# Twelve rounds of zero products between the biases' products and the first x products of a GRU kernel

## The chip, the cores and the metric

The kernel runs on one core of a Trainium2 chip. The metric is the device time of one execution in microseconds. The runs of the kernel before took 1161.91, 1162.43 and 1162.65 us, a median of 1162.43. TensorE (PE) does the matrix products, and its weight loads are shown as an engine of their own (PEld). VectorE (DVE), ScalarE (ACT) and GpSimd (POOL) do the elementwise work. SyncE (SP), ACT and POOL issue the transfers.

## The reference

x has 16 sequences of 256 steps with 512 values. A GRU runs over the steps with one state of 512 values for each sequence. An expert layer with top-k choice over all 4096 tokens follows, and its result is added to x.

```python
def cell(h, x):
    gi = x @ W_ih + b_ih
    gh = h @ W_hh + b_hh
    i_r, i_z, i_n = jnp.split(gi, 3, axis=-1)
    h_r, h_z, h_n = jnp.split(gh, 3, axis=-1)
    r = jax.nn.sigmoid(i_r + h_r)
    z = jax.nn.sigmoid(i_z + h_z)
    n = jnp.tanh(i_n + r * h_n)
    h_new = (1.0 - z) * n + z * h
    return (h_new, h_new)
...
logits = xf @ router_w + router_b
S = jax.nn.softmax(logits, axis=-1)
G, idx = jax.lax.top_k(S.T, k)
tokens = xf[idx]
out = jnp.einsum('ekh,hd->ekd', tokens, expert_w) + expert_b
weighted = G[..., None] * out
y = jnp.zeros((bs, h), dtype=x.dtype).at[idx.reshape(-1)].add(weighted.reshape(-1, h))
...
x = x + ffn(gru(cond_2048, x))
```

Both stages are in float32. Each step needs the state of the step before it, so the 256 steps run one after another.

## The kernel before

**Tiling.** The 512 columns of a gate are split into four parts of 128 (KC = 4). A product for 16 or 32 rows uses 32 columns of the TensorE array, so four of them, one for each quadrant j, stand side by side and write to PSUM partitions 32j to 32j + 31. Steps are taken in pairs p, with an even and an odd step sharing 32 PSUM rows. Each pair has banks of its own out of six (`banks`): `ra` for the r gate and the x part of the n gate, `hn` for the h part of n, `zz` for the z gate. Eight steps make a group g.

**Set-up, before the loop.** The transfers are issued in an order written out by hand (lines 276 to 299). SP and ACT each load half of the rows of `wih` and then of `whh`, by gate in the order r, n, z. POOL loads the biases, then the first two x pairs of group 0 into `xa0`, then the first state into `c0`. SP loads the remaining two x pairs behind its halves of the weights.

On PE and DVE the order is also written by hand, in the block that the change touches. PE runs, in this order:

1. `begin_sums` (line 108) for the six banks: four products of zeros each, bfloat16, 128 rows and 512 columns. They set every bank to zero and open it for sums.
2. `keep_clock(22)`: 22 rounds of `begin_sums` on two spare PSUM banks, `idles`, which nothing reads.
3. `biases(1)` and `biases(0)` (line 303): the bias rows are spread over the quadrants by products with a column of ones. They have only one or two rows to sum over. DVE copies the result to `bias` and `nb`, from which later pairs are preset.
4. The x products of pairs 0 and 1, `x_part` (line 436): first the r and n parts with 256 columns, then the z part with 128, for four blocks k each. They read `xT`, which DVE transposes from `xa0` by `turn_x` (line 253), one pair at a time.
5. `keep_clock(2)`: two more rounds.

Meanwhile DVE transposes the first state and copies it to `hs` (lines 492 and 493).

**The loop.** For every step s, PE runs the h products (`h_part`, line 450: r and n for the first half of k, r and n for the second half, then z). ACT and DVE then work out the gates and the new state, which the next step's h products need. PE fills the wait with the x products of later pairs and with units of the expert layer. In step 1, DVE transposes the rest of `xa0`; after that, group 1's x is loaded into the same buffer. What follows the loop is the softmax, the search for the k-th largest score, and the sums and stores of the output.

Of the kernel before, what the change touches and what calls it, by code (L numbers as in the profile page):

```python
# [18 lines left out]
def kernel(  # L19
# [88 lines left out]
    def begin_sums(bank):  # L108

        n = bank.shape[-1]  # L110
        for j in range(KC):
            nc.tensor.matmul(
                bank[QD * j : QD * (j + 1)],
                zero,
                zero[:, 0:E].unsqueeze(1).to_broadcast([P, n // E, E]),
                start=True,
                stop=True,
                tile_position=(0, QD * j),
            )
# [67 lines left out]
    with (  # L187
# [65 lines left out]
        def turn_x(g, xa, pairs=slice(0, TG // 2)):  # L253
            if g not in xT:
                xT[g] = xtp.tile([P, TG // 2, P], F32, name="xt")
            nc.vector.transpose(  # L256
                xT[g][:, pairs, :].rearrange("p q (c r) -> p q c r", c=KC),
                xa[:, pairs, :].rearrange("p q (i c) -> p q c i", c=KC),
            )
# [43 lines left out]
        def biases(i):  # L303
            for dst, rows in (
                (ra[i][:, 0, :], b_raw[:, 0, :]),
                (ra[i][:, 1, :], b_raw[0:1, 2, :]),
                (hn[i][:, 0:P], b_n),
                (zz[i], b_raw[:, 1, :]),
            ):
                for j in range(KC):  # L310
                    nc.tensor.matmul(
                        dst[quadrant(j)],
                        ones[0 : rows.shape[0]],
                        columns(rows, j),
                        start=False,
                        stop=True,
                        tile_position=(0, QD * j),
                        skip_group_check=True,
                    )
# [3 lines left out]
        def of_step(ap, odd):  # L323
            return ap.rearrange("p (c q b) -> p c q b", q=2, b=B)[:, :, odd, :]
# [111 lines left out]
        def x_part(p, k, z):  # L436
            g, pair = divmod(p, TG // 2)
            lhs = xT[g][:, pair, QD * k : QD * (k + 1)]
            for j in range(KC):
                q = quadrant(j)  # L440
                dst, rhs = (
                    (zz[p % 2][q], columns(wih[:, k, 2, :], j))
                    if z
                    else (ra[p % 2][q], columns(wih[:, k, 0:2, :].rearrange("p g d -> p (g d)"), j))
                )
                nc.tensor.matmul(  # L446
                    dst, lhs, rhs, start=False, stop=(k == KC - 1), tile_position=(0, QD * j), skip_group_check=True
                )
# [22 lines left out]
        def keep_clock(n):  # L471

            for i in range(n):
                begin_sums(idles[i % 2])

        with tc.manual_schedule(engines={ET.PE, ET.DVE}):
            for bank in banks:
                begin_sums(bank)
            keep_clock(22)
            biases(1)  # L480
            biases(0)
            nc.vector.tensor_copy(bias[:, 0:2, :], ra[1])
            nc.vector.tensor_copy(nb, hn[1][:, 0:P])
            nc.vector.tensor_copy(bias[:, 2, :], zz[1])
            for pair in range(2):
                turn_x(0, xa0, slice(pair, pair + 1))
            for z in (False, True):
                for pair in range(2):
                    for k in range(KC):
                        x_part(pair, k, z)  # L490
            keep_clock(2)
            nc.vector.transpose(turned, c0)
            nc.vector.tensor_copy(hs[:, :, 0, :], of_step(turned, 0))
# [400 lines left out]
```

## Time and profile before

| | |
|---|---|
| median of 3 runs | 1162.43 us (1161.91 to 1162.65) |
| the profiled execution, its own time | 1162.4 us |
| its span, first to last instruction | 1160.5 us |
| mean granted TensorE clock | 0.996 |
| zero rounds of `keep_clock(22)`, last product ends | 9.29 us |
| biases' products (L311), PE | 9.22 to 11.18 us |
| x products of pairs 0 and 1 (L446), PE | 15.49 to 22.56 us |
| h products of step 0 (L459), PE | from 22.82 us |
| ACT's sigmoid of r in step 0 (L517) | 24.38 us |

Times within the execution are counted from the first instruction. A row of the timeline gives the start, the length, the engine, the line, the operation with its tiles (out<-in) and shapes, and how many instructions it merges; in brackets is the idle time of the engine before it and what ended it. A row of the table by stretches gives the stretch, its length, the busy time of PE, PEld, DVE, ACT and POOL with the number of instructions, then the granted TensorE clock as a share of full speed (PEclk), the share of the transfer engines and their GB/s. Each float32 product counts as two MATMUL instructions. Their ends are modelled, so their starts and the weight loads are the surer measure.

### The profile page before, as it was taken

To read this page: it belongs to the slowest core of one execution; us is meant where nothing else is said; L and a number is where in the kernel's file an instruction comes from. 1 tells how busy PE (TensorE), PEld (TensorE's weight loads), DVE (VectorE), ACT (ScalarE), POOL (GpSimd) and SP (SyncE) were. 2 spreads that over 40 slices of the span, in tenths; PEclk is the share of its full clock that TensorE was granted. 3 is DMA by queue.
4 is the path that set the end of the run, shared out by engine and by line. 5 is a ranking of instruction groups with operands and counts; after the bars stand their busy time and mean duration, and the time that the engine had idled before them with its cause. 6 is when DMAs were issued, how large, how long until landed. Compare 5 with 4: busy or idle time off the path is not lost. (4 is left out here: it accounts for less than half of the span.)

```text
span 1160.5 us, 79363 instructions
## 1 busy us (share of the span) xinstructions
PE 1145.6 (99%) x36017; PEld 1008.8 (87%) x36017; DVE 703.4 (61%) x4078; ACT 343.2 (30%) x1459; POOL 100.0 (9%) x412
## 2 busy tenths in 40 slices
PE   7999999999999999999999999999999999999998
PEld 4899999999999999999999999999999999989742
DVE  1656665666666566666665666666666666666675
ACT  0323323232333333333233322233232323343320
POOL 3000010000000000000000000000000000000000
PEclk8999999999999999999999999999999999999999
DMA  7200000000000000000000000000000000000017
GB/s 235 73 23 20 21 18 21 21 20 19 20 21 20 21 20 20 21 20 21 20 19 22 21 20 18 23 20 21 18 21 20 20 21 20 21 18 13 4 45 249
DMA packets 48854, 38.01 MB, mean 33 GB/s; under 512 B 7968, under 2 KB 40800, under 8 KB 48512
## 3 DMA queue, kind: packets, MB, share of 16 engines
q1 hardware_dynamic: 46272, 29.56, 8.6%
q8 instruction: 283, 4.64, 1.7%
q10 hardware_dynamic: 1632, 3.15, 0.8%
q14 instruction: 59, 0.48, 0.1%
q0 software_dynamic: 608, 0.19, 0.1%
HBM read 24.47 MB, written 8.39 MB: 28 GB/s over the span
## 5 line engine op out<-in xcount | busy, mean ns | idle before, releaser
L459 PE MATMUL gates<-whh,hs 128*16 128x128 f32 x24576 | 719.4, 273 | 3.5 <-DVE hs L592 2.0
L459 PEld LDWEIGHTS gates<-whh,hs 128*16 128x16 f32 x24576 | 672.2, 103 | 10.0 <-DVE hs L592 4.6
L446 PE MATMUL gates<-wih,xt 128*32 128x256 f32 (+1 forms) x8192 | 380.9, 327 | 4.4 <-DVE xt L256 4.3
L446 PEld LDWEIGHTS gates<-wih,xt 128*32 128x32 f32 x8192 | 245.2, 110 | 72.4 <-DVE xt L256 4.6
L517 ACT ACTIVATE r<-gates 128x128 f32<-128x128 f32 x256 | 70.9, 277 | 605.5 <-PE gates L459 605.5
L521 DVE COPY seen<-r 1x1 f32<-1x1 f32 x256 | 36.3, 142 | 326.8 <-ACT r L517 326.8
L571 ACT ACTIVATE t<-t 128x64 f32<-128x64 f32 x512 | 102.9, 248 | 132.6 <-DVE t L569 132.6
L578 DVE STREAM_TRANSPOSE nT<-t 128x64 f32<-128x64 f32 x512 | 100.2, 234 | 49.3 <-ACT t L571 49.3
L581 DVE STREAM_TRANSPOSE zT<-zs 128x64 f32<-128x64 f32 x512 | 121.7, 238 | 0.2 <-issue 0.2
L592 DVE TENSOR_TENSOR hs<-v,nT 128x32 f32<-128x32 f32 x512 | 101.7, 199 | 21.7
L589 DVE TENSOR_TENSOR v<-u,zT 128x32 f32<-128x32 f32 x512 | 104.4, 204 | 8.8
L407 PE MATMUL pe<-ewr,ht 128*32 128x128 f32 x1920 | 93.9, 273 | 0.0
L567 DVE TENSOR_TENSOR t<-r,gates 128x64 f32<-128x64 f32 x512 | 89.7, 217 | 0.0
L569 DVE TENSOR_TENSOR t<-t,gates 128x64 f32<-128x64 f32 x512 | 88.4, 214 | 0.0
L584 DVE TENSOR_TENSOR u<-hs,nT 128x32 f32<-128x32 f32 x512 | 78.4, 153 | 0.0
L407 PEld LDWEIGHTS pe<-ewr,ht 128*32 128x32 f32 x1920 | 59.5, 110 | 19.4
L572 ACT ACTIVATE zs<-gates 128x128 f32<-128x128 f32 x256 | 70.9, 277 | 0.0
L137 PE MATMUL pe<-ewr,ht 128*32 128x256 f32 (+1 forms) x848 | 64.3, 442 | 0.0
L622 POOL COPY xa<-hs 32x1 f32<-32x1 f32 x120 | 21.4, 179 | 478.7 <-DVE hs L592 296.7
L331 POOL COPY ht<-hs 128x128 f32<-128x128 f32 (+1 forms) x128 | 46.9, 397 | 160.2 <-DVE hs L592 152.4
L247 POOL COPY xs<-hs 1x1 f32<-1x1 f32 x128 | 22.7, 178 | 335.7 <-DVE hs L592 331.4
L137 PEld LDWEIGHTS pe<-ewr,ht 128*32 128x32 f32 x848 | 26.0, 109 | 26.2 <-issue 17.4
(102 smaller groups left out, 316.7 us busy)
## 6 DMA issues: line engine op xcount, KB each, us to landing
xs<-in_x_dram SPq DMA_DIRECT2D x128, 64.0 KB
xa<-in_x_dram SPq DMA_DIRECT2D x248, 32.0 KB
out_dram<-xs SPq DMA_DIRECT2D x31, 256.0 KB
wih<-in_L_cond_W_ih_dram SPq DMA_DIRECT2D x3, 512.0 KB
wih<-in_L_cond_W_ih_dram ACTq DMA_DIRECT2D x3, 512.0 KB
whh<-in_L_cond_W_hh_dram SPq DMA_DIRECT2D x3, 512.0 KB
whh<-in_L_cond_W_hh_dram ACTq DMA_DIRECT2D x3, 512.0 KB
ewr<-in_L_ffn_expert_w_dram SPq DMA_DIRECT2D x1, 1024.0 KB
```

Source lines behind the costliest of these rows:

```text
L137: nc.tensor.matmul(pe[q, cols], ht[:, g, k, q], ewr[:, k, E:][:, cols], start=False, stop=(k == KC - 1), tile_position=(0, QD * j), skip_g ...
L407: nc.tensor.matmul(pes[g][quadrant(j), at : at + P], ht[:, g, k, quadrant(j)], ewr[:, k, E + P * quarter : E + P * (quarter + 1)], start=F ...
L446: nc.tensor.matmul(dst, lhs, rhs, start=False, stop=(k == KC - 1), tile_position=(0, QD * j), skip_group_check=True)
L459: nc.tensor.matmul(dst[quadrant(j, m)], lhs, columns(whh[:, k, gate_, :], j), start=False, stop=(k == KC - 1), tile_position=(0, QD * j), ...
L567: nc.vector.tensor_tensor(t[half], r[:, cols], hn[p % 2][:, cols], ALU.mult)
L569: nc.vector.tensor_tensor(t[half], t[half], ra[p % 2][:, 1, cols], ALU.add)
L571: nc.scalar.activation(t[half], t[half], AF.Tanh)
L578: nc.vector.transpose(nT[half], t[half])
L581: nc.vector.transpose(zT[half], zs[:, halves[half][1]])
L584: nc.vector.tensor_tensor(u[half], hs[:, halves[half][2], slot(s), :], of_step(nT[half], odd), ALU.subtract)
L589: nc.vector.tensor_tensor(v[half], u[half], of_step(zT[half], odd), ALU.mult)
L592: nc.vector.tensor_tensor(hs[:, halves[half][2], slot(s + 1), :], v[half], of_step(nT[half], odd), ALU.add)
```

## The change

One line is added between the biases' products and the first x products, behind DVE's copies of the biases. PE's own order has the twelve rounds directly behind the last bias product. A round is `begin_sums` on one of the two spare banks, as in the 22 rounds before the biases.

```diff
@@ -482,6 +482,7 @@
             nc.vector.tensor_copy(bias[:, 0:2, :], ra[1])
             nc.vector.tensor_copy(nb, hn[1][:, 0:P])
             nc.vector.tensor_copy(bias[:, 2, :], zz[1])
+            keep_clock(12)
             for pair in range(2):
                 turn_x(0, xa0, slice(pair, pair + 1))
             for z in (False, True):
```

The functions it calls are unchanged:

```python
def keep_clock(n):
    for i in range(n):
        begin_sums(idles[i % 2])

def begin_sums(bank):
    n = bank.shape[-1]
    for j in range(KC):
        nc.tensor.matmul(
            bank[QD * j : QD * (j + 1)],
            zero,
            zero[:, 0:E].unsqueeze(1).to_broadcast([P, n // E, E]),
            start=True,
            stop=True,
            tile_position=(0, QD * j),
        )
```

`zero` is a tile of bfloat16 zeros that POOL sets once, at the start.

## The prediction

> **What bounds the kernel now.** I read the page first, for the engines and the clock. TensorE (PE) is busy for 99% of the span, the next engine for 61%. The chain of waits on the page breaks off after the last output transfer, so the order of the start has to be read from the timeline.
>
> ```profile
> PE 1145.6 (99%) x36017; PEld 1008.8 (87%) x36017; DVE 703.4 (61%) x4078; ACT 343.2 (30%) x1459; POOL 100.0 (9%) x412
> ...
> PEclk8999999999999999999999999999999999999999
> ```
>
> The reader is to see that nearly all of the run is one serial recurrence on TensorE, so time gained before its first step is kept to the end. The only slice with a granted clock below nine tenths is the first, 0 to 29 us, where the change is. Next the PE timeline there (start, us, line, tiles, count), then the DVE rows that release it:
>
> ```profile
> 9.22 1.96 PE L311 MATMUL gates<-xs,ones 2*32 2x128 f32 x64
> 15.49 7.07 PE L446 MATMUL gates<-wih,xt 128*32 128x256 f32 x128 [4.30 <-DVE xt L256]
> 22.39 0.61 PE L112 MATMUL idle<-zero 128*32 128x512 bf16 x8
> ```
>
> ```profile
> 15.03 0.40 DVE L256 STREAM_TRANSPOSE xt<-xa 128x128 f32<-128x128 f32 x1 [4.28 <-DMA xs<-in_cond_dram]
> 15.97 0.41 DVE L256 STREAM_TRANSPOSE xt<-xa 128x128 f32<-128x128 f32 x1 [0.54 <-DMA xa<-in_x_dram]
> ...
> 18.75 0.20 DVE L493 COPY hs<-nT 128x64 f32<-128x64 f32 x1
> ```
>
> After the biases' products PE has nothing to do for 4.30 us, until the first x pair is transposed. From 15.49 on, nothing but PE itself sets the end of this stretch: the second pair and the first state (18.95) are ready before PE asks for them. Last, the granted clock (PEclk is the third column from the end) over the clock's own stretches, and the weight loads, whose spacing shows the speed:
>
> ```profile
> 8.67:12.08 3.41, 2.51 (x76) 1.81 (x68) 0.82 (x3) 1.28 (x1) 2.77 (x7) 1.00 1.06 312
> 12.08:15.50 3.42, 0.01 (x2) 0.01 (x3) 0.40 (x1) 0.00 (x0) 1.51 (x6) 0.50 1.07 332
> 15.50:18.91 3.41, 3.41 (x34) 1.58 (x37) 0.89 (x4) 0.00 (x0) 0.00 (x0) 0.50 1.05 378
> 18.91:22.32 3.41, 3.41 (x100) 2.64 (x96) 0.99 (x8) 0.00 (x0) 0.30 (x1) 1.00 0.67 235
> ...
> 25.74:29.15 3.41, 2.30 (x85) 2.33 (x89) 1.89 (x14) 0.50 (x2) 0.17 (x1) 1.00 0.16 45
> ```
>
> ```profile
> 18.05 0.20 PEld L446 LDWEIGHTS gates<-wih,xt 128*32 128x32 f32 x4 [0.23 <-issue]
> 18.48 0.20 PEld L446 LDWEIGHTS gates<-wih,xt 128*32 128x32 f32 x4 [0.23 <-issue]
> 18.90 3.39 PEld L446 LDWEIGHTS gates<-wih,xt 128*32 128x32 f32 x92 [0.23 <-issue]
> ```
>
> The clock falls to half at 12.08 and comes back at 18.91, two equal stretches of 3.41 us later. So the first 3.4 us of the x products run at half speed: four loads every 0.43 us.
>
> **The change, part by part.** It adds 12 rounds of four 128x512 products, 48 of PE's 36017 matmuls, and removes and moves nothing. No semaphore of another engine stands before them: they read the zero tile and write the idle banks that the 22 rounds before have used. The DVE copies of the biases (9.93 to 10.75) run beside them. SP, ACT and POOL get no instruction, so no transfer is issued earlier or later by the change itself.
>
> *Length of the rounds.* At full speed the row "5.16, 3.64 us, x68" of the weight loads before the biases gives 3.64 / 17 = 0.214 us a round, and at half speed the rows at 4.73 and 5.16 are 0.43 apart. The bias products stop issuing at about 11.0 (loads 9.22 + 1.69, plus the last product). Twelve rounds end at 11.0 + 12 x 0.214 = 13.6 if the clock holds. If it falls at 12.08 as now, five rounds are done by then and seven take 7 x 0.43 = 3.0 us, to 15.1. Both are before 15.48, where the x products can first start. The rounds therefore cost nothing while that idle time covers them; without it they would cost 2.6 to 5.1 us.
>
> *Speed of the x products.* They are 16 passes of 256 columns, then 16 of 128. Now eight wide passes take 0.427 us (15.49 to 18.90), the other eight 0.2135 and the narrow ones 0.107: 3.42 + 1.71 + 1.71 = 6.84 us. At full speed from the start they take 16 x 0.2135 + 16 x 0.107 = 5.13 us. The gain is **1.71 us**. The second x pair, transposed at 16.38, is first asked for at 15.49 + 8 x 0.2135 = 17.20.
>
> *Does the clock hold?* This is the unknown. Two answers give the full gain: it never falls, or it falls at 12.08 and the seven half-speed rounds win it back at 15.50. What no row shows is a stretch of 3.41 us about half full of zero rounds. From above: the stretch at 25.74 held PE work for 2.30 of 3.41 us and the clock stayed. From below: the one at 8.67 held 2.51 us, and it fell; but 1.9 us of that are bias products with two of 128 rows in use, and only about 0.6 us are zero rounds. I take it that such products count for little. With the change the stretch to 12.08 holds 0.6 + 1.1 us of rounds, 50%. If the clock holds there, the next holds 1.5 us, 44%; if it falls there, the next is filled to 3.0 of 3.41, 88%. For comparison the first stretch of the run, 1.84 to 5.26, was full, and the clock was at full speed afterwards by the spacing of the loads. The ends are 0 and 1.71 us. I take 1.71, because the 88% case is near a row that won the clock back and the 50% case is nearer to 67% that held than to 18% that fell.
>
> Here a rule has to be weighed. The Trainium skill, "TensorE: Matmul & The Clock Gate", section "What's actually happening", lets the clock fall only after a whole idle window of about 3.4 us, and rise after about 3.4 us of sustained work. The trace agrees on the length (3.41 us) but not on the first half: the clock fell 0.9 us after the last bias product. By the page no window after the change is idle, so the gain is 1.71. By the row a half-filled stretch may fall too, and then the x products are slow again: gain 0. The second half of the rule speaks against the change as well: rounds that last 2.6 us at full speed, or leave 0.4 us of the stretch empty at half speed, are not a whole window of work. By its letter a clock that has fallen at 12.08 stays down to 18.91, gain 0.
>
> *What is late next.* The h products of step 0 start 1.71 us earlier, at 22.82 - 1.71 = 21.11, after the old two rounds. They need the state (18.95, early enough) and whh. In slices of 0.2 us, the ACT queue's (q10) last packets are these; in 22.8 to 23.0 it has none:
>
> ```profile
> q10 hardware_dynamic: 2, 0.00, 2.9%
> ```
>
> That row is of 22.6 to 22.8. The z block is the last to load and the last third of the step. Its loads are now at 22.60 + 64 x 2.73 / 96 = 24.4, and its ACT half at 24.9. With the change they are due at 22.7 and 23.2. The SP queue's half can't be told from x packets on the same queue. The cost of this wait lies between 0 and 1.7 us (now there is no wait at 24.4, so the weights have landed by then). By the row I put the landing at 22.9: a wait of about 0.2. ACT's sigmoid of z (25.69) starts as its tanh ends, so hardly any of it is hidden; I take **0.15**.
>
> From there on it is the same recurrence, shifted. SP's first later load (24.60) waits for its own queue, but its data is first used many steps later. The transfer that makes DVE wait for 1.4 us before 40.62 is issued after the transpose at 31.53, so it shifts as well.
>
> **Sum.** -1.71 + 0.15 = -1.56 us against the profiled execution's own time of 1162.4 (span 1160.5 and 1.9 around it): 1160.84. The runs' median of 1162.43 is the same within 0.03, so the forecast is **1160.8**, 0.13% less. About 0.2%, or 2.3 us, is what a measurement of this kernel can tell from no change. The forecast lies inside it.
>
> **Rivals.**
> 1. *The clock is at half speed anyhow*, because a half-filled stretch isn't enough. For it: the fall at 12.08 with PE not idle. Against: what filled that stretch were two-row products. Time 1162.4.
> 2. *The gain waits for whh.* The h products start earlier, but the weights land at 23.5 or later. For it: the weights' load is the longest transfer of the start, and a few packets of it trickle until 22.8. Against: those packets end before the z block is due by the loads' spacing, give or take 0.2. Most of the gain goes: 1161.6 to 1162.4.
> 3. *Slower: the rounds run into the x products.* The place is PE's queue ahead of L446. All twelve at half speed last 12 x 0.427 = 5.1 us, to 16.1, and x starts 0.65 late. With the clock back at 18.91, 6.5 wide passes are done by then, and the rest takes 9.5 x 0.2135 + 1.71 = 3.74, to 22.65: +0.37, 1162.8. With the clock back only at 22.33 it is +2.1, 1164.5; one stretch later still +4.1, 1166.5. It passes 0.2% only if the clock is back after 22.33. Against: it was full for 1.1 us after the biases in this trace.
> 4. *A larger gain.* If the clock's stretches lie otherwise against the start in other executions, the half-speed part of the x products in the runs before can be longer than 3.4 us. With 5 us of it the gain is 2.5: 1159.9. Against: the three runs spread over 0.74 us only, and the profiled one is at their middle.
>
> **How the numbers follow.** Forecast 0.60 (own range 1160.2 to 1161.5; 0.04 of it below 1160.1), rival 1 0.16, rival 2 0.06, rival 3 0.07 (0.05 beyond 0.2%), rival 4 0.11. So faster 0.04 + 0.11 = 0.15, slower 0.05, within 0.2% 0.80. The range goes from rival 4's edge, 1159.9, to rivals 1 and 2 with the runs' scatter, 1162.7.
>
> **What would show it.** Right: the loads of the x products 0.21 apart from 15.5 on, PEclk 1.00 from 15.50, h products starting near 21.1, mean clock 0.998 or more. If the clock fell and came back, the rounds' loads are 0.43 apart from 12.08 on. Rival 1 shows 0.50 in 15.50 to 18.91. Rival 2 shows PE idle inside step 0, before the z block. Rival 3 shows an L446 product starting after 15.6. The forecast is wrong if the products start at 21.1 and the end has not moved: then something later ties the recurrence to a transfer.

## The result, and the profile after

The changed kernel takes 1161.26 us (median of 20 runs, 1160.65 to 1162.53). The kernel before, run beside it, takes 1162.98 us (20 runs, 1161.79 to 1164.58). The ratio is 0.9986, with a 95% interval of 0.9979 to 0.9992: 1.72 us less, or 0.14%. The profiled execution took 1161.04 us, its span 1159.2 us. Two later measurements of the same kernel give 0.9987 (0.9980 to 0.9993) and 0.9986 (0.9979 to 0.9992).

The page of the changed kernel, the rows of engines and clock:

```profile
PE 1147.5 (99%) x36065; PEld 1010.1 (87%) x36065; DVE 703.7 (61%) x4078; ACT 343.4 (30%) x1459; POOL 99.7 (9%) x412
...
PEclk9999999999999999999999999999999999999999
```

There are 48 MATMUL instructions more, as the diff says, and the first slice of the clock is now at nine tenths or above. The PE timeline of the changed kernel at the start:

```profile
9.88 1.96 PE L311 MATMUL gates<-xs,ones 2*32 2x128 f32 x64
11.77 2.78 PE L112 MATMUL idle<-zero 128*32 128x512 bf16 x48
15.28 5.41 PE L446 MATMUL gates<-wih,xt 128*32 128x256 f32 x128 [0.73 <-DVE xt L256]
20.50 0.62 PE L112 MATMUL idle<-zero 128*32 128x512 bf16 x8
20.94 2.80 PE L459 MATMUL gates<-whh,hs 128*16 128x128 f32 x96
```

The rounds end before the x products can start, and the x products' row is 5.41 us where it was 7.07. Step 0's h products start at 20.94, against 22.82 before: 1.88 us earlier. 0.21 of that is the x data, which came earlier in this execution. By stretches, with the borders at which the clock changed before:

```profile
8.67:12.08 3.41, 3.41 (x96) 2.31 (x92) 0.82 (x3) 1.28 (x1) 3.26 (x8) 1.00 1.07 318
12.08:15.50 3.42, 2.69 (x52) 1.14 (x48) 0.42 (x2) 0.00 (x0) 1.09 (x6) 1.00 1.06 337
15.50:18.91 3.41, 3.41 (x72) 2.10 (x68) 1.87 (x10) 0.00 (x0) 0.30 (x1) 1.00 1.05 377
```

PEclk is 1.00 in all three; before it was 0.50 in two. Later the shift against the kernel before changes. I took it at ACT's sigmoid of r in every step. It is 1.88 us at step 0, 2.88 at step 5, 1.69 at step 6 and 1.82 at step 255. Two events lie behind that. The 1.36 us for which DVE waited for x before 40.62 are gone in this profile, and something new stands in step 5. The PE, DVE and ACT rows of the changed kernel there:

```profile
40.77 1.94 PE L459 MATMUL gates<-whh,hs 128*32 128x128 f32 x60
43.54 1.18 PE L459 MATMUL gates<-whh,hs 128*32 128x128 f32 x34 [0.83 <-issue]
```

```profile
43.99 0.35 DVE L568 TENSOR_TENSOR t<-r,gates 128x64 f32<-128x64 f32 x2 [1.18 <-PE gates L459]
```

```profile
42.36 0.28 ACT L518 ACTIVATE r<-gates 128x128 f32<-128x128 f32 x1 [2.01 <-PE gates L459]
47.56 0.28 ACT L518 ACTIVATE r<-gates 128x128 f32<-128x128 f32 x1 [2.42 <-PE gates L459]
```

From here on a count of products is one of MATMUL instructions. After 60 of the 96 products of step 5, PE stops for 0.83 us and waits for nothing that the profile shows ("issue"). The row behind the stop has 34 of the remaining 36; the last two start among the next x products and have a row of their own. I go by the row behind the stop, here and below, and call its count the products left. DVE waits for the missing products, and the step lasts 5.20 us where 4.0 is usual. In the transfers of 41.0 to 41.5 us stands one packet of the instruction queue, 16 KB:

```profile
q8 instruction: 1, 0.02, 12.0%
```

In this trace such packets start 3.5 to 5 us apart in the loop, but the one before started at 34.8 and this one only at 41.2. It had landed at 42.17, and PE went on at 43.54. Between the two packets the 1 MB transfer of the experts' weights is issued (34.89).

### The profile page after: what moved, and what is told of

Same layout as the page of the kernel before. It is cut to its first block, busy times and chain, and to the rows that moved or that the text cites. A ratio compares the mean times of both kernels' runs of the same rounds, so it can differ in the third digit from the quotient of the medians.

```text
span 1159.2 us, 79459 instructions
## 1 busy us (share of the span) xinstructions
PE 1147.5 (99%) x36065; PEld 1010.1 (87%) x36065; DVE 703.7 (61%) x4078; ACT 343.4 (30%) x1459; POOL 99.7 (9%) x412
```

## The experiments

My theory for the start: the granted clock follows how much of each stretch of 3.41 us is filled with products that use all rows. The rounds fill it, and the x products run at full speed. The rival: any work on TensorE counts, and only an idle stretch lets the clock fall. For step 5: PE runs out of instructions, because a block of them comes in behind a large transfer; the added products moved the end of a block into step 5's h products. The rival: it has nothing to do with the added work.

**The kernel before, once more.**

> The kernel before, unchanged, for a second profile and the clock of every run. Theory (the clock is judged over stretches of 3.41 us that run free of the kernel's start): the stretch borders lie elsewhere than 5.26, 8.67 and 12.08, the clock still falls between 9.5 and 16 us and is back between 16 and 21 us, so the x products start at half speed for 0.9 to 5 us; the mean clock of the runs lies between 0.996 and 0.998. Rival (the borders hang on the start of the kernel): the fall is at 12.08 and the return at 18.91 again, give or take 0.1. Time the same as before within 0.3 us.

Measured: 1162.67 us, ratio 1.0003 (0.9994 to 1.0011). Its PE row and weight loads, and the stretches of its own clock:

```profile
15.25 8.34 PE L446 MATMUL gates<-wih,xt 128*32 128x256 f32 x128 [4.61 <-DVE xt L256]
```

```profile
20.80 0.20 PEld L446 LDWEIGHTS gates<-wih,xt 128*32 128x32 f32 x4 [0.23 <-issue]
21.23 2.09 PEld L446 LDWEIGHTS gates<-wih,xt 128*32 128x32 f32 x68 [0.23 <-issue]
```

```profile
14.42:17.83 3.41, 2.58 (x27) 1.20 (x31) 0.82 (x2) 0.00 (x0) 0.00 (x0) 0.50 1.06 369
17.83:21.24 3.41, 3.41 (x38) 1.57 (x34) 1.46 (x9) 0.00 (x0) 0.30 (x1) 0.50 0.88 318
```

The borders lie elsewhere: the fall is at 11.00 and the return at 21.24, three stretches later. A stretch filled to 2.58 of 3.41 us (76%) did not win the clock back. The x products ran at half speed for 14 passes, 5.98 us, where the first profile had 8. The stretches run free of the kernel's start. The return, the 5.98 us and the mean clock of this execution, 0.994, all lie outside what I expected, since I had not allowed for a third stretch at half speed.

**Two rows.** In place of the twelve rounds the same 48 products with two of the 128 rows:

```diff
-            keep_clock(12)
+            for i in range(12):
+                for j in range(KC):
+                    nc.tensor.matmul(
+                        idles[i % 2][QD * j : QD * (j + 1)],
+                        zero[0:2],
+                        zero[0:2, 0:E].unsqueeze(1).to_broadcast([2, D // E, E]),
+                        start=True,
+                        stop=True,
+                        tile_position=(0, QD * j),
+                    )
```

> The twelve rounds in the same place and of the same length (2.6 us at full speed), but with two of 128 rows, as the biases' products have. Theory (the clock asks for rows in use, and two-row products count for next to nothing): the clock falls as in the kernel before, the x products start at half speed, time within 0.5 us of before. Rival (any work on TensorE keeps the clock): clock 1.00 to the x products, time 1.7 us below before, as the changed kernel.

Measured: 1163.37 us, ratio 1.0008 (1.0000 to 1.0017). By stretches:

```profile
9.84:13.26 3.42, 3.42 (x100) 2.65 (x100) 0.82 (x3) 1.28 (x1) 3.11 (x10) 1.00 1.07 329
13.26:16.67 3.41, 3.41 (x37) 1.33 (x32) 0.81 (x2) 0.00 (x0) 0.00 (x0) 0.50 1.06 342
```

PE was busy for the whole stretch to 13.26, only with two-row products, and the clock fell at its end. Busy time does not keep the clock; the rival is out. The gain is gone. The median is 0.95 us above that of before, more than the 0.5 I allowed, though the interval reaches down to no difference. The profile has the stop in step 5 here too, for 1.15 us, so this kernel has that loss without the gain.

**Fewer and more rounds**: `keep_clock(4)`, `keep_clock(8)`, `keep_clock(24)`.

> Four full-row rounds in place of twelve: 0.86 us of work, so about 2.7 us or more stay empty before the x products. Theory (a stretch of 3.41 us has to be filled to some share, above a fifth and below two thirds, whatever its longest gap): the clock falls in most executions, and the time is 0 to 0.9 us below before. Rival (only a whole idle stretch of about 3.4 us makes the clock fall): no stretch is wholly idle, the clock holds, and the time is 1.7 us below before.

> Eight rounds in place of twelve: 1.7 us of work, 1.7 to 2.4 us left empty before the x products. Theory (a stretch filled to about half holds the clock, and the position of the block of instructions moves with the number of added products): where TensorE runs out in step 5, 18 products of 96 are left (34 less 16); the clock holds in most executions; time 1.0 to 2.0 us below before. Rival (a half-filled stretch lets the clock fall): x products at half speed for part of their time, time 0 to 0.8 us below before.

> Twenty-four rounds: 5.1 us at full speed, past the point where the first x products could start (15.3 to 15.5). Theory (rounds are free only as long as they lie in the idle time; the clock holds): the first L446 product starts at 16.1 to 16.9, 0.7 to 1.6 us late, at full speed, and the time is 0.1 to 1.0 us below before. Rival (the gain isn't the clock but something else about the added work, such as a shifted instruction stream): no relation to the start of L446; the time is 1.7 us or more below before.

Measured: four rounds 1162.67 us, ratio 1.0002 (0.9993 to 1.0010); eight 1161.91, 0.9996 (0.9987 to 1.0004); twenty-four 1162.18, 0.9998 (0.9989 to 1.0006). Two stretches with four rounds and two with eight, then the x products' PE row with twenty-four:

```profile
12.28:15.70 3.42, 0.26 (x7) 0.17 (x10) 0.40 (x1) 0.00 (x0) 1.51 (x6) 1.00 1.06 332
15.70:19.11 3.41, 3.41 (x39) 1.73 (x35) 1.32 (x7) 0.00 (x0) 0.30 (x1) 0.50 1.06 381
```

```profile
11.67:15.09 3.42, 1.15 (x24) 0.32 (x12) 0.00 (x0) 0.03 (x1) 1.56 (x7) 1.00 1.07 332
15.09:18.50 3.41, 2.92 (x28) 1.38 (x32) 0.98 (x3) 0.00 (x0) 0.00 (x0) 0.50 1.05 369
```

```profile
17.02 5.38 PE L446 MATMUL gates<-wih,xt 128*32 128x256 f32 x128
```

With four rounds the stretch that matters is nearly empty and the clock falls at 15.70. With eight, the last round in the stretch to 15.09 starts at 12.44; with its 0.21 us the rounds fill 0.98 us of the stretch, or 29%, and the clock falls too. (PE's own column has 1.15, as ends of products are modelled.) The return is quicker there: 2.92 of 3.41 us (86%) won the clock back. The mean clocks of the 13 runs say that eight rounds are at the edge: five have 0.999 and take 1160.85 to 1161.49 us, like the changed kernel, and eight have the 0.997 or 0.998 of the kernels whose clock fell and take 1161.43 to 1165.13. I had expected the clock to hold in most executions. The times with four rounds and with eight missed their ranges as well; neither differs from before clearly. With twenty-four the clock holds and the x products take the same 5.4 us, but start at 17.02, slightly later than the 16.9 I had allowed, and most of the gain is given away.

**The changed kernel twice more.**

> The changed kernel again, beside the next three on the same chip. Theory (the clock holds to the x products, 1.7 to 1.9 us gained there; then TensorE runs out of instructions in step 5, where a block of instructions has to come in behind the 1 MB transfer of the experts' weights): the x products' loads are 0.21 apart, step 5 is 0.5 to 1.7 us longer than its neighbours with an idle TensorE put down to issue, 34 products of that step's 96 left; time 1.2 to 2.2 us below before.

> The changed kernel, as the measure for the three below on the same chip. Theory: 1.2 to 2.2 us below before; step 5 stretched by 0.5 to 1.7 us with 34 products left.

Measured: 1161.27 us against 1162.57 (21 and 49 runs), and 1161.26 against 1162.88 (21 and 62). In both profiles the clock held and PE stopped with 34 products of step 5 left, for 0.85 and 1.44 us. In the first of them DVE waited for x as well (in the second for 0.48 us):

```profile
38.10 1.17 DVE L256 STREAM_TRANSPOSE xt<-xa 128x512 f32<-128x512 f32 x1 [1.06 <-DMA xa<-in_x_dram]
```

So that wait is not gone with the change; it comes and goes between executions.

The second of these profiles has the tightest case of a return, in the zero products at the very start. Its weight loads:

```profile
3.02 0.16 PEld L112 LDWEIGHTS <-zero 128*32 128x32 bf16 x4 [0.26 <-issue]
3.45 4.50 PEld L112 LDWEIGHTS <-zero 128*32 128x32 bf16 x84 [0.26 <-issue]
```

The loads are 0.43 us apart up to 3.45 and without a pause behind it. The products begin at 0.92, and the border of this profile's stretches lies at 3.56: 2.64 of 3.41 us (77%) sufficed.

**Where the block ends.** Three rounds of float32 zeros (`zero_f`, from a zero tile of double width) last as long as the twelve, with 24 MATMUL instructions in place of 48:

```diff
-            keep_clock(12)
+            zero_f = zeros.bitcast(F32)
+            for i in range(3):
+                for j in range(KC):
+                    nc.tensor.matmul(
+                        idles[i % 2][QD * j : QD * (j + 1)],
+                        zero_f,
+                        zero_f[:, 0:E].unsqueeze(1).to_broadcast([P, D // E, E]),
+                        start=True,
+                        stop=True,
+                        tile_position=(0, QD * j),
+                    )
```

> The same 2.6 us of zero rounds in place of the twelve, as three rounds of float32 zeros: four times the time a product, with two instructions where bfloat16 has one, so 24 products in place of 48. Theory (the clock only asks for filled rows; the position of TensorE's blocks of instructions moves with the number of products): clock held; where TensorE runs out in step 5, 10 products are left (34 less 24) in place of 34, the stall is 0.3 to 0.8 us shorter, and the time is 0.2 to 0.8 us below the changed kernel. Rival (the stall hangs on time alone, not on the number of instructions): the stall as in the changed kernel with about 34 products left, time equal.

Measured: 1161.76 us, ratio 0.9986 (0.9979 to 0.9993). That is the changed kernel's time within the noise, not the 0.2 to 0.8 us below it that I expected. The PE row at the stop, then those with twenty-four rounds and with eight:

```profile
46.51 0.52 PE L460 MATMUL gates<-whh,hs 128*32 128x128 f32 x10 [1.62 <-issue]
```

```profile
44.56 2.49 PE L459 MATMUL gates<-whh,hs 128*32 128x128 f32 x82 [1.45 <-issue]
```

```profile
45.16 0.74 PE L459 MATMUL gates<-whh,hs 128*32 128x128 f32 x18 [0.29 <-issue]
```

The products left are 10, 82 and 18, against 34 with twelve rounds: 34 - 24, 34 + 48 and 34 - 16. With four rounds it is the weight loads that pause, for 0.39 us, with 2 left: 34 - 32. The two-row run, with 48 added products, stops with 34 left. The count from the first product of the kernel says the same: in each of these profiles, and in all three of the changed kernel, 988 products have started when PE stops, whatever was added. The stop hangs on the number of products ahead of it, and the rival is out. Its length does not follow the position: 1.62 us with 10 left, 0.83 to 1.44 with 34. My hope for a shorter stop with fewer instructions was wrong. The float32 profile has a second stop, 0.31 us in step 0 with 83 products left. From there to its stop in step 5 there are 639 products, five times 128 but for one.

**Moving the large transfer.** First, the experts' weights, the router's and the two biases are issued ahead of group 1's x:

```diff
-            for j in range(KC):
-                load_xa(1, xa1, j, (nc.sync, nc.sync))
             nc.sync.dma_start(out=ewr[:, :, E:], in_=expert_w.rearrange("(c p) n -> p c n", c=KC))
...
+            for j in range(KC):
+                load_xa(1, xa1, j, (nc.sync, nc.sync))
```

> The changed kernel, with the experts' and router's weights and the two last biases issued on SP ahead of group 1's x, so that they move at 24 to 29 us and not at 37 to 43 us. Theory (the stall in step 5 is an instruction block held up by that transfer): no idle TensorE put down to issue in steps 4 and 5, no transpose waiting for x; 1.0 to 1.7 us below the changed kernel, 2.5 to 3.5 us below before. Rival (the stall comes with any block of instructions, whatever else moves): the stall stays, with 34 products left, and the time is that of the changed kernel within 0.4 us. A second rival (group 1's x, now later on the queue, becomes late): the transpose in step 3 waits, and the time is above the changed kernel's.

> The same move in the kernel before, without the added rounds. Theory: the half speed of the x products stays (0.9 to 2.6 us lost), the waits of steps 4 and 5 go: 0.3 to 1.0 us below before. The difference to the changed kernel with the same move is then the rounds' own worth, 1.7 to 2.3 us, more than in the pair without the move. Rival (the move gains nothing): equal to before.

Measured: with the rounds 1161.14 us, ratio 0.9988 (0.9980 to 0.9997), as without the move, where I had expected 1.0 to 1.7 us less; in the kernel before 1162.43, ratio 0.9995 (0.9987 to 1.0003), not clearly changed. The PE row of the first:

```profile
31.96 1.38 PE L459 MATMUL gates<-whh,hs 128*16 128x128 f32 x42 [1.03 <-issue]
```

Step 5 ran without a stop, and step 2 had one instead. PE stops after 605 products in place of 988. The 383 between are three times 128 but for one. The instruction packets had their gap at 20.95 to 29.69 us, around the transfer's new time (issued at 24.21). So the late block went with the transfers that were moved. The router's weights and the biases moved along, so this does not say yet which of them delays it. In the kernel before, no step stopped in this profile.

Then the 1 MB went in four pieces of 256 KB:

```diff
-            nc.sync.dma_start(out=ewr[:, :, E:], in_=expert_w.rearrange("(c p) n -> p c n", c=KC))
...
+                if 3 <= s < 3 + KC:
+                    k = s - 3
+                    nc.sync.dma_start(out=ewr[:, k, E:], in_=expert_w[k * P : (k + 1) * P, :])
```

> The changed kernel with the 1 MB of experts' weights in four transfers of 256 KB, issued in steps 3 to 6, one a step. Theory (a block of TensorE's instructions waits behind whatever large transfer is queued at its time; moved early as one piece, the transfer held up the block of step 2, with 42 loads left): no piece is large enough to hold a block for long, all of steps 2 to 6 last 3.9 to 4.1 us but for at most 0.4 us in one, and the time is 0.6 to 1.3 us below the changed kernel. Rival (the block comes late whatever is queued): 0.5 us or more of idle TensorE put down to issue in one of these steps, time as the changed kernel.

> The same spread in the kernel before. Theory (before, the waits of steps 3 to 6 take back what an execution lost at the start, or cost by themselves): they go, so 0.2 to 1.0 us below before, and the changed kernel with the spread is 1.7 to 2.6 us below this one, which is what the clock is worth at the start of the recurrence. Rival (the rounds are worth what they show in the pair without the spread): the difference is 1.0 to 1.5 us.

Measured: 1161.00 us, ratio 0.9986 (0.9979 to 0.9993), and 1162.66, ratio 0.9994 (0.9986 to 1.0003). The stop stays where it was, and my theory that the single piece is at fault falls:

```profile
46.66 1.18 PE L458 MATMUL gates<-whh,hs 128*32 128x128 f32 x34 [1.10 <-issue]
```

Two of the pieces, a bias of 256 KB and several loads of x are still issued between 39 and 44 us, around this block. Which of them delays it was not separated. The pair's difference is 1.66 us, about what it is without the spread, and between what theory and rival had forecast.

Of the profiles with twelve rounds, the changed kernel's with the spread (1161.00 us) alone shows the rounds fail. The profiled execution took 1163.89 us, one of two of the kernel's 18 runs above 1161.4. Its stretches:

```profile
10.63:14.05 3.42, 3.42 (x76) 1.69 (x68) 0.33 (x2) 1.24 (x1) 3.18 (x11) 1.00 1.05 347
14.05:17.46 3.41, 1.20 (x26) 0.70 (x26) 0.83 (x2) 0.00 (x0) 0.38 (x2) 0.99 1.08 339
17.46:20.87 3.41, 3.41 (x40) 1.74 (x36) 1.38 (x9) 0.00 (x0) 0.30 (x1) 0.51 1.01 366
```

The x data came late and the x products started at 16.33. The stretch ends at 17.42, so it was filled to 1.09 us (32%), and the clock fell in the middle of the x products. The mean clock of this execution is 0.998. Three of the 62 runs of the changed kernel itself have that value too (1161.28, 1161.41 and 1164.08 us); the others have 0.999 or 1.000.

No version was clearly faster than the changed kernel.

## Why the prediction was right

- **The bound and the place.** Right: the gain is made ahead of step 0 and most of it reaches the end. Wrong is "the same recurrence, shifted". The unchanged kernels' profiles (two before, three after) have their first sigmoid of r at 24.90 and 22.49 us in the mean, a gain of 2.41. From step 4 to step 8 the gain falls to 1.32, where the stop for instructions and the wait for x lie, and stays there; the last step brings it to 1.50, for a reason that I did not look for. So 0.9 us is given back in all. I had looked only at data transfers there. That the added products move the ends of the instruction blocks was in no step of mine.
- **The rounds lie in idle time.** Right in all three profiles: their weight loads end at 14.05, 13.73 and 12.68, and the x products start at 15.28, 14.87 and 15.58. The price without that cover is the run with twenty-four.
- **The speed of the x products, 1.71 us.** The mechanism is right: 5.1 us of loads in each of the three. The size was that of one execution. The half-speed part before was 8 and 14 passes in the two profiles of the kernel before, and 12 and 9 in the two with moved transfers and no rounds. At 0.2135 us a pass that is 1.71, 2.99, 2.56 and 1.92 us, 2.3 in the mean. What I gave as the fourth rival, borders that lie otherwise, is the rule; it did not reach the end as a larger gain because of what is given back. One size in the third rival is off: with the clock back one stretch after 22.33, three of the narrow passes still run at full speed, so it would have been +3.8 and not +4.1 us.
- **Does the clock hold?** I chose rightly between the row and the rule of the Trainium skill, page "TensorE: Matmul & The Clock Gate", section "What's actually happening". Its idle window is too strict for a fall: stretches filled to 8, 29 and 32% let it fall, none of them wholly idle. Its sustained work is too strict for a rise: 77% sufficed, while 76% did not. In the changed kernel's three profiles, with each product counted from its start for as long as the next one of its kind takes to follow, full-row work filled 42% or more of each stretch up to the x products but one. That one held with 38%, beside two-row products. In the second profile of the kernel before, the stretch to 11.00 had 29% beside as much two-row work, and fell. So the rounds hold the clock with little to spare where the borders lie badly. That half a stretch would do was a guess of mine from two far rows, and it came out right.
- **The wait for whh, 0.15 us.** Wrong: step 0's h products take 2.80 us, 2.79 before, without a gap. The weights had come in time.
- **The sum.** -1.56 forecast, -1.72 measured. Errors cancel: in the mean of the profiles the gain at the start is 0.7 larger than the 1.71 and the 0.15 for whh is not paid, but 0.9 is given back later. That the number came so close is luck in part.

## What to carry to other kernels

The stretches over which the clock falls and returns run free of the kernel's start, so one profile does not price them: here the half-speed part was 8 to 14 passes. Take several. Filler work counted by the rows it used, not by its time, and had to fill more than a third of every stretch up to the real work. Added instructions also move the ends of the instruction blocks, and if one that comes late ends up in a serial chain, part of the gain goes there.

## What was not expected

- The clock fell after 3.4 us of uninterrupted two-row products, and held through stretches filled with full-row products to 36% (the stretch to 12.28 with four rounds, beside two-row products) and 48% (the third profile of the changed kernel, with nothing beside). It fell at 32%. So in these traces the bound for a fall lies near a third. Before a return, 2.52 and 2.58 us of 3.41 did not suffice and 2.64, 2.85 and 2.92 did: that bound lies near 77%.
- TensorE's instructions come in blocks of about 128 products with their weight loads, 16 KB each: the profile before has 283 such packets for 36017 products. In all ten profiles with added products a block came late and held up the weight loads inside a step's h products, for 0.39 to 1.89 us. In each of the ten the loads go on 1.2 to 1.5 us after the late packet has landed. In the four without added products that never happened there. In one of these (spread transfer) PE stopped for 0.17 us in the x products behind step 5's h products, with 28 of their 40 to come, 12 past the end of the h products. That is where the count puts it: with 48 products fewer ahead, the 36 to come in the changed kernel's step 5 become 36 - 48 = -12. What makes the packet late is open.
